# A fused residual kernel: LoRA tables and parked x on GpSimd's DMA queue, the convolution in groups of 8 channels, nine places for the first weights

## The chip, the cores and the metric

The kernel runs on one core of one Trainium2 chip. The metric is the device time in microseconds (us) of one execution; the median of several runs is compared.

## The reference, cut to what matters

`x` has shape 32 x 64 x 1024 (samples B, channels H, positions L), all in float32. Four stages each add their result to `x`:

```
x = x + conv(x)     # per channel h: causal convolution over L with a kernel K[h] made from
                    # exp, sin and 64 states per channel, plus D[h]*x, masked by each sample's length
x = x + x @ W1[id1[b]].T      # 1024 x 1024 weights chosen per sample out of 16
x = x + x @ W2[id2[b]].T      # the same, other weights
gate = x @ Wg.T + 0.5 * (x @ Ag[id3[b]].T) @ Bg[id3[b]].T      # 1024 -> 2752, rank-16 LoRA per sample
up   = x @ Wu.T + (the same with Au, Bu)
x = x + down(silu(gate) * up)                                  # 2752 -> 1024, with Ad, Bd
```

## The kernel before, in words

**Places.** `x` is kept transposed, positions on the partitions, in four chunks of 8 samples (`xs[0..3]`, 2 MB each). Chunks 2 and 3 lie in `x2pool` on the right-hand side of SBUF only until they are stored to DRAM ("parked", tile `xd`, line 129); they are loaded again later (tile `x`, line 462). All big weights go through `wpool`, nine places of 512 KB (`wa` for W1 and W2, `wf` for gate and up, `wd` for down). `early` (line 122) has four more places of 512 KB which the first four weight loads take instead, and which are used only once.

**Order of the work.** TensorE's order is the order in which the program is written (`manual_schedule(engines={PE})`). The other queues are ordered by a planner at build time, which takes the instruction written earliest among those that are ready in its own estimate; `tc.issue_after(ins)` adds that an instruction of the same queue comes after `ins`. Inside one queue everything is issued in order, and an instruction that has to wait holds up what is behind it.

**Convolution (lines 577 to 833).** `kernels(g)` makes the convolution kernels of a group of channels: GpSimd makes the products of lines 738 and 739, ScalarE takes exponentials and sines, VectorE does the range reduction and products (lines 620 to 626 and 758 to 762), TensorE multiplies 32 x 32 blocks (`pk`, line 766), ScalarE copies them to `ks` (774), VectorE adds D to one element of each (776), and two stores write them to DRAM (`kp`, 778 and 779). `convolve` takes four channels: the SP queue loads the input `uf` (787) and, for each two channels, a 1 MB Toeplitz tile `hk` out of `kp` (792); TensorE multiplies (`pc`, 804), VectorE masks into `tmp` (812), GpSimd adds into the four chunks (820). The groups are 8, 8, 16, 16 and 16 channels, and the kernels of a group are made when the convolution of the group before it has 12 channels left, or after its first four if it has 8 channels.

**Weights W1 and W2 (lines 159 to 227).** `adapters(c)` walks through one chunk: for each pair of samples and each of the two layers, 16 loads `wa` (185) and TensorE's product `pa` (191); ScalarE copies the result to `y` (201), TensorE transposes it back (`py`, 210), VectorE adds it to `x` (214). It is a generator: `yield` hands over after each half of a product (8 loads). Chunk 0 runs alone after the convolution; chunks 1 to 3 are laid between the pieces of the feed-forward of the chunk before. The loads of the first piece of chunk 0 are issued after the sixth `hk` load (line 559).

**Feed-forward (lines 369 to 557).** For each chunk, `prepare` loads the LoRA tables of gate and up (`columns`: eight DMAs on ScalarE's queue, line 259, into `raw`; one copy to `at`, line 264), forms `pl_g` and `pl_u` (285) and the combinations `xd` of `x` (362 to 366, 442). `gated` does one block of 128 hidden units: `bgu` is gathered by GpSimd (234), expanded on TensorE to `pe` (328) and copied by ScalarE to `lt` (338), which gives four PSUM banks back; then 2 x 7 half-size products `pf` (386). The result goes to `act` (421). `between` is called after each half. The table of down (`raw_d`) is also loaded by `columns`, at the start of each block of hidden units; the down products are `po` (515).

**At the seam** between chunk 0's adapters and its feed-forward, ScalarE's queue holds in this order: the last two copies of `y`, the two stores of `park` (129), the copy `at_u`, the eight loads of `raw_d`, and then the copies `lt`.

Of the kernel before, what the change touches and what calls it, by code (L numbers as in the profile page):

```python
# [8 lines left out]
F32 = mybir.dt.float32  # L9
# [2 lines left out]
ALU = mybir.AluOpType  # L12
PE = mybir.EngineType.PE
SP = mybir.EngineType.SP
ACT = mybir.EngineType.Activation

P = 128
B, H, L = 32, 64, 1024
# [7 lines left out]
FM = (FH + P - 1) // P  # L26
BLOCKS = ((0, 6), (6, FM))
MB = 6
EARLY = 4
SEG = 3  # L30
TH = TC // 2
KH = KT // 2
# [1 line left out]
NE = 16  # L34
NPIECE = 2 * BC
AT_GATED, AT_DOWN = 4, 5
GROUPS = (8, 8, 16, 16, 16)
HG = max(GROUPS)
LQ = 32
KROW = P + L  # L40

# [22 lines left out]
def kernel(  # L64
# [52 lines left out]

    right = ExitStack()
    x2pool = right.enter_context(tc.tile_pool(name="x2pool", bufs=1, side="right"))
    epool = right.enter_context(tc.tile_pool(name="epool", bufs=1, side="right"))  # L120
    late = [x_tile(x2pool, c, f"x{c}") for c in range(2, NCK)]
    early = [epool.tile([P, L], F32, tag=f"e{i}", name=f"early{i}") for i in range(EARLY)]
    blocks = convolution(tc, cst, consts, xt, xf, ssm, lens, xs + late, ps_tile)
# [2 lines left out]
    def park():  # L126
        for c, x_c in enumerate(late, 2):
            d = dpool.tile([P, KT, TC], F32, tag=f"xd{c}", name=f"xd{c}")
            nc.scalar.dma_start(d, x_c)
            parked.append(d)  # L130

    ids_sb = cpool.tile([1, 3 * B], I32, tag="ids", name="ids_sb")
# [20 lines left out]

    loads, copies = [], []
    ypool = ctx.enter_context(tc.tile_pool(name="ypool", bufs=2, reuse_waits="tile"))

    def adapter(w, layer, b0, pending):
        c, lo = b0 // BC, (b0 % BC) * H  # L160
        es = []
        for b in (b0, b0 + 1):
            with ExitStack() as after:
                if len(loads) > 1:

                    after.enter_context(tc.issue_after(loads[-2]))
                es.append(
                    nc.values_load(
                        ids_sb[0:1, layer * B + b : layer * B + b + 1],
                        engines=[SP],  # L170
                        min_val=0,
                        max_val=NE - 1,
                    )
                )
        acc = [acc_tile(f"pa{layer}_{b0}_{i}") for i in range(2)]
        for kt in range(KT):
            if kt == KH:
                yield
            if kt == (c == 0) and pending:
                residual(*pending.pop())  # L180
            wts = []
            for s, e in enumerate(es):
                name = f"wa{layer}_{b0 + s}_{kt}"
                wt = early.pop(0) if early else wpool.tile([P, L], F32, tag="w", name=name)
                load = nc.sync.dma_start(
                    wt, w[bass.ds(e, 1), kt].rearrange("e p f -> p (e f)")
                )
                wts.append(wt)
            for i in range(2):
                for s in range(2):  # L190
                    nc.tensor.matmul(  # L191
                        acc[i][s * H : (s + 1) * H, :],
                        xs[c][:, kt, lo + s * H : lo + (s + 1) * H],
                        wts[s][:, i * 512 : (i + 1) * 512],
                        start=(kt == 0),
                        stop=(kt == KT - 1),
                    )
        loads.append(load.ins)
        y = ypool.tile([P, L], F32, tag="y", name=f"y{layer}_{b0}")
        for i in range(2):  # L200
            copy = nc.scalar.copy(y[:, i * 512 : (i + 1) * 512], acc[i])
        copies.append(copy.ins)
        pending.append((c, lo, y, f"{layer}_{b0}"))
        yield

# [10 lines left out]
    def adapters(c):  # L216

        pending = []  # L220
        n = BC // 2
        for i in range(n + 1):
            if i < n:
                yield from adapter(w1, 0, c * BC + 2 * i, pending)
            if i > 0:
                yield from adapter(w2, 1, c * BC + 2 * i - 2, pending)
        residual(*pending.pop())

    hpool = ctx.enter_context(tc.tile_pool(name="hpool", bufs=1, reuse_waits="tile"))
    gpool = ctx.enter_context(tc.tile_pool(name="gpool", bufs=2, reuse_waits="tile"))  # L230

    def gather(table, c, piece, width, tag, name, bufs):
# [8 lines left out]
        )  # L241
        return t

    cols = []

    def columns(table, c, n, name):

        raw = gpool.tile([P, BC, n, R], F32, tag="raw", name=f"raw_{name}", bufs=1)
        for b in range(BC):
            with ExitStack() as after:  # L250
                if len(cols) > 3:
                    after.enter_context(tc.issue_after(cols[-4]))
                e = nc.values_load(
                    ids_sb[0:1, 2 * B + c * BC + b : 2 * B + c * BC + b + 1],
                    engines=[ACT],
                    min_val=0,
                    max_val=NE - 1,
                )
            load = nc.scalar.dma_start(
                raw[:, b], table[bass.ds(e, 1)].rearrange("e p n r -> (e p) n r")  # L260
            )
            cols.append(load.ins)
        t = gpool.tile([P, n, BC, R], F32, tag="at", name=f"at_{name}", bufs=1)
        nc.scalar.copy(t, raw.rearrange("p b n r -> p n b r"))
        return t.rearrange("p n b r -> p n (b r)")
# [94 lines left out]
        return a11, a12, s4, a22, s1, s2, a21  # L360

    def moving(b11, b12, b21, b22, t1, t2, t3, t4):
        nc.vector.tensor_sub(t3, b22, b12)
        nc.vector.tensor_sub(t1, b12, b11)
        nc.vector.tensor_sub(t2, b22, t1)
        nc.vector.tensor_sub(t4, b21, t2)
        return b11, b21, b22, t4, t1, t2, t3

    def gated(c, m, xb, between):
# [46 lines left out]
            cs.append(cq)  # L416
            between(2 * m + g)

        act = apool.tile([P, 2, TC], F32, tag="act", name=f"act_{c}_{m}")
        a = act[:n].rearrange("p i (t n) -> p (i t) n", t=2)  # L420
        nc.scalar.activation(a, cs[0][:n], AF.Sigmoid)
        nc.vector.tensor_mul(a, a, cs[0][:n])
# [23 lines left out]
    def ffn(c, xb, others):  # L446
# [10 lines left out]
                due[1] += 1  # L457

        def between(i):
            if i == 0 and c and c + 1 < NCK:  # L460
                x_n = x_tile(xpool, c + 1, "x")
                nc.sync.dma_start(x_n, parked[c - 1])
                xs.append(x_n)
            other(AT_GATED)

        for block, (m0, m1) in enumerate(BLOCKS):
# [19 lines left out]
            ab = []  # L486
            for i, act in enumerate(acts):
                k = k_of(m0 + i)
                t3 = apool.tile([P, 4, TH], F32, tag="actd", name=f"actd_{c}_{m0 + i}")
                q = [act[:k, h, t * TH : (t + 1) * TH] for h in (0, 1) for t in (0, 1)]  # L490
                ab.append(moving(*q, *(t3[:k, j] for j in range(4))))

# [63 lines left out]
                    other(AT_DOWN)  # L556
        return ready

    with tc.issue_after(blocks[5]):

        pieces = adapters(0)
        next(pieces)
    for _ in pieces:
        pass
    with tc.issue_after(copies[-1]):
        park()
    right.close()
    apool = ctx.enter_context(
        tc.tile_pool(name="apool", bufs=MB, side="right", reuse_waits="tile")
    )  # L570
    prepare(0, "g")
    xb = prepare(0, "u")
    for c in range(NCK):
# [3 lines left out]
def convolution(tc, cst, consts, xt, xf, ssm, lens, xs, ps_tile):  # L577
# [9 lines left out]
    with ExitStack() as ctx:  # L587
# [25 lines left out]
        def tt(o, a, b, op):  # L613
            nc.vector.tensor_tensor(o, a, b, op)  # L614
            return o
# [100 lines left out]

        def kernels(g):

            h0, hg = sum(GROUPS[:g]), GROUPS[g]
            shape = [P, hg, LQ]  # L720

            def over_l(ap):
                return ap[:, h0 : h0 + hg].unsqueeze(2).to_broadcast(shape)

            def over_h(at):
                return cst[:, at : at + LQ].unsqueeze(1).to_broadcast(shape)
# [2 lines left out]

            def big(tag, pool=s1):  # L730
                n[0] += 1
                return pool.tile([P, HG, LQ], F32, tag=f"b{tag}", name=f"b{tag}{g}_{n[0]}")[
                    :, :hg
                ]

            def powers(at, tag):
                theta, rho = big(f"th{tag}"), big(f"rho{tag}")
# [24 lines left out]
            tt(gt, p1, rho1, ALU.mult)  # L762

            ps = ps_tile(f"pk{g}")
            for i in range(hg):
                nc.tensor.matmul(
                    ps[:LQ, i * LQ : (i + 1) * LQ],
                    gt[:, i, :],
                    et[:, i, :],
                    start=True,  # L770
                    stop=True,
                )
            ks = s2.tile([LQ, HG, LQ], F32, tag="ks", name=f"ks{g}")[:, :hg]
            nc.scalar.copy(ks.rearrange("a h b -> a (h b)"), ps[:LQ, : hg * LQ])
            k0 = ks[0:1, :, 0]
            tt(k0, k0, dskip[0:1, h0 : h0 + hg], ALU.add)
            kp = dram.tile([hg, KROW], F32, tag=f"kp{g}", name=f"kp{g}")
            nc.scalar.dma_start(kp[:, :P], zero[:hg])
            nc.scalar.dma_start(kp[:, P:].rearrange("h (a b) -> a h b", b=LQ), ks)
            return kp  # L780

# [1 line left out]

        def convolve(kp, row, ha):

            uf = s3.tile([P, 4, KT, B], F32, tag="uf", name=f"uf{ha}")
            nc.sync.dma_start(uf, xf[:, ha : ha + 4])
            tmp = s2.tile([P, 4, KT * B], F32, tag="tmp", name=f"tmp{ha}")
            for i in range(0, 4, 2):
# [30 lines left out]
                nc.gpsimd.tensor_tensor(xv, xv, tv[:, :, c * BC : (c + 1) * BC, :], ALU.add)  # L820


        ready = kernels(0)
        ha = 0
        for g, hg in enumerate(GROUPS):
            nxt = None
            for row in range(0, hg, 4):
                convolve(ready, row, ha)
                ha += 4
                if row == max(hg - 12, 0) and g + 1 < len(GROUPS):  # L830
                    nxt = kernels(g + 1)
            ready = nxt
        return loads


# [131 lines left out]
```

## Time and profile before

| | |
|---|---|
| median of 3 runs | 2477.97 us (2476.69 to 2479.43) |
| the profiled execution's own time | 2475.95 us |
| its span in the trace | 2474.2 us |
| TensorE matmul busy | 2393.5 us (97%) |
| VectorE / ScalarE / GpSimd busy | 1116.5 / 344.5 / 130.8 us |
| moved by DMA | 500.54 MB, mean 202 GB/s |

"Busy" is the time in which an engine has an instruction running; issuing a DMA does not count. For TensorE it also holds time in which a matmul in the pipeline waits. A line of a view by groups or in order of time names the line of the program, the engine, the operation, what is written from what (`pf<-xd,wf`), the shapes and how many instructions it stands for; `SPq`, `ACTq` and `POOLq` are the queues in which an engine issues DMAs.

### The profile page before, as it was taken

What the parts mean: (1) busy time and instruction counts of PE and PEld (TensorE: products, weight loads), DVE (VectorE), ACT (ScalarE), POOL (GpSimd) and SP (SyncE); (2) the same over time, 40 slices, a digit from 0 to 9 for tenths busy, and PEclk for the clock granted to TensorE, in tenths of its full rate; (3) what the DMA queues carried; (4) which work ended last, traced back from release to release, by engine and by line L of the source; (5) the groups of instructions that cost most, each with busy time, mean ns of one, the idle gap of its engine ahead of it and who ended that gap; (6) DMA issues with size and microseconds to landing.
All of it is one profiled execution on the core that took longest, in us unless ns stands there. A gap on an engine that the chain in (4) does not pass through costs nothing.

```text
span 2474.2 us, 35037 instructions
## 1 busy us (share of the span) xinstructions
PE 2393.5 (97%) x13600; PEld 1804.0 (73%) x13600; DVE 1116.5 (45%) x2127; ACT 344.5 (14%) x656; POOL 130.8 (5%) x136
## 2 busy tenths in 40 slices
PE   3899998999999999999999999999999999999999
PEld 3895335777777787777777687777777688888887
DVE  9611003444344554444345454445345546554554
ACT  4100001111011111111011111111011102110110
POOL 3431000000000000000000000000000000000000
PEclk9999999999999999999999999999999999999999
DMA  6789997656566547655665547555655543223221
GB/s 247 253 290 356 409 409 268 246 183 225 174 225 229 183 125 261 225 204 197 203 217 212 175 139 268 213 200 203 210 206 204 181 152 117 88 69 109 94 63 62
DMA packets 176184, 500.54 MB, mean 202 GB/s; under 512 B 19794, under 2 KB 69266, under 8 KB 174994
## 3 DMA queue, kind: packets, MB, share of 16 engines
q1 hardware_dynamic: 146338, 461.82, 52.8%
q10 hardware_dynamic: 25584, 22.85, 2.8%
q0 software_dynamic: 4096, 13.63, 1.7%
q8 instruction: 107, 1.75, 0.3%
q14 instruction: 59, 0.48, 0.1%
HBM read 485.36 MB, written 12.88 MB: 201 GB/s over the span
## 4 chain that ended last, share of the span: by engine, by line
PE 88%; DMA 8%; DVE 4%; issue 0%; ACTq 0%; SPq 0%; POOL 0%; ACT 0%; DVEq 0%
PE pf L386 42%; PE po L515 22%; PE pa L191 14%; DMA wa<-in_w 5%; PE pc L804 5%; PE pe L328 2%; PE py L210 1%; PE pl_d L285 1%; DMA xd<-x 1%; PE po L311 1%; DMA x<-xd 1%; DMA out_y<-x 0%; DVE bk L620 0%; DVE bsp L614 0%; DMA wf<-in_wu 0%; PE pl_u L285 0%
## 5 line engine op out<-in xcount | busy, mean ns | idle before, releaser
L386 PE MATMUL pf<-xd,wf 128*128 128x256 f32 (+1 forms) x2816 | 670.0, 382 | 8.9 <-ACT lt L338 8.9
L386 PEld LDWEIGHTS pf<-xd,wf 128*128 128x128 f32 (+1 forms) x2816 | 523.8, 188 | 108.2 <-issue 9.7
L386 PE MATMUL pf<-xd,s 128*128 128x256 f32 (+1 forms) x2112 | 500.5, 380 | 0.3 <-DVE s L357 0.3
L191 PE MATMUL pa<-wa,x 128*64 128x512 f32 x2032 | 482.9, 598 | 12.4 <-DMA wa<-in_w 8.5
L386 PEld LDWEIGHTS pf<-xd,s 128*128 128x128 f32 (+1 forms) x2112 | 396.6, 188 | 61.9 <-issue 0.7
L191 PEld LDWEIGHTS pa<-wa,x 128*64 128x64 f32 x2032 | 147.8, 136 | 312.6 <-issue 248.6
L515 PE MATMUL po<-act,wd 128*128 128x256 f32 x704 | 177.0, 385 | 0.0
L804 PE MATMUL pc<-uf,hk 128*128 128x256 f32 (+7 forms) x1024 | 154.3, 315 | 21.1 <-DMA hk<-kp 11.9
L515 PE MATMUL po<-actd,s 128*128 128x256 f32 x704 | 173.0, 379 | 0.1
L515 PE MATMUL po<-actd,wd 128*128 128x256 f32 x704 | 172.9, 379 | 0.0
L804 PEld LDWEIGHTS pc<-uf,hk 128*128 128x128 f32 x1024 | 149.9, 197 | 25.4 <-issue 15.2
L411 DVE TENSOR_TENSOR c<-pf,u 128x256 f32<-128x256 f32 (+1 forms) x88 | 37.3, 424 | 266.5 <-PE pf L386 266.5
L515 PEld LDWEIGHTS po<-act,wd 128*128 128x128 f32 x704 | 130.3, 190 | 31.5 <-issue 8.3
L515 PEld LDWEIGHTS po<-actd,s 128*128 128x128 f32 x704 | 133.5, 190 | 18.9 <-DVE s L357 0.6
L515 PEld LDWEIGHTS po<-actd,wd 128*128 128x128 f32 x704 | 133.6, 190 | 18.4
L234 POOL DMA_INDIRECT bgu<-in_bgu,rows x44 | 46.9, 1066 | 1809.3 <-PE pe L328 1690.8
L338 ACT COPY lt<-pe 128x512 f32<-128x512 f32 (+1 forms) x176 | 90.4, 598 | 277.9 <-PE pe L328 142.1
L356 DVE TENSOR_TENSOR s<-wf 128x512 f32<-128x512 f32 x88 | 60.7, 690 | 128.9 <-DMA wf<-in_wu 56.1
L415 DVE TENSOR_TENSOR c<-c,lt 128x1024 f32<-128x1024 f32 (+1 forms) x88 | 107.5, 1222 | 5.1 <-DVE c L413 0.5
L214 DVE TENSOR_TENSOR x<-py,x 128x512 f32<-128x512 f32 x64 | 42.9, 688 | 144.1 <-PE py L210 143.9
L356 DVE TENSOR_TENSOR s<-wd 128x384 f32<-128x384 f32 x64 | 33.4, 522 | 141.5 <-PE po L515 96.7
L409 ACT COPY c<-pf 128x256 f32<-128x256 f32 (+1 forms) x88 | 32.8, 372 | 417.4 <-PE pf L386 417.4
(148 smaller groups left out, 1671.2 us busy)
## 6 DMA issues: line engine op xcount, KB each, us to landing
wa<-in_w SPq DMA_DIRECT2D x508, 512.0 KB, 7.0
wf<-in_wg SPq DMA_DIRECT2D x88, 512.0 KB, 4.0
wf<-in_wu SPq DMA_DIRECT2D x88, 512.0 KB, 4.3
wd<-in_wd SPq DMA_DIRECT2D x96, 384.0 KB, 4.1
hk<-kp SPq DMA_DIRECT2D x32, 1024.0 KB, 7.6
x<-in_xt SPq DMA_DIRECT2D x4, 2048.0 KB, 13.4
uf<-in_xf SPq DMA_DIRECT2D x16, 512.0 KB, 7.7
wd<-in_wd SPq DMA_DIRECT2D x32, 256.0 KB, 3.1
```

The source lines that it names most:

```text
L191: nc.tensor.matmul(acc[i][s * H : (s + 1) * H, :], xs[c][:, kt, lo + s * H : lo + (s + 1) * H], wts[s][:, i * 512 : (i + 1) * 512], start= ...
L214: nc.vector.tensor_add(cols, ps, cols)
L234: nc.gpsimd.indirect_dma_start(out=t, out_offset=None, in_=table, in_offset=bass.IndirectOffsetOnAxis(ap=rows[:, c, piece : piece + 1], axis=0
L328: nc.tensor.matmul(ps[:n, at_ : at_ + 2 * H], bt[pair(j), g, i, :n], tms["gu"[g]][pair(j)], start=(g + i == 0), stop=True, skip_group_chec ...
L338: nc.scalar.copy(lt[:n, :, 2 * H * j : 2 * H * (j + 1)], ps[:n].rearrange("p (i t) -> p i t", i=4),)
L356: nc.vector.tensor_add(s1, a21, a22)
L386: nc.tensor.matmul(ps, ws[j][:, kt, :n], xb[j][:, kt, :], start=start and kt == 0, stop=kt == KH - 1, skip_group_check=True,)
L409: nc.scalar.copy(cq[:n, 0], pa)
L411: nc.vector.tensor_add(cq[:n, 1], pb, u[:n])
L415: nc.vector.tensor_add(cf, cf, lt[:n, g].rearrange("p i t -> p (i t)"))
L515: nc.tensor.matmul(pss[j], ws[j][:k, i, :], ab[m - m0][j], start=(m == m0 and home[j] % 2 == 0), stop=(m == m1 - 1), skip_group_check=True,)
L804: nc.tensor.matmul(ps[:, j, d * B :], hk[:, j, d * P : (d + 1) * P], uf[:, i + j, : KT - d, :].rearrange("p k b -> p (k b)"), start=(d == ...
```

## The change

- `park` issues its two stores on GpSimd's queue, not ScalarE's, and is called later: inside `between`, after the first half of the first `gated`, after the last table load issued so far. The pool `apool` of `act` and `actd`, which takes the places of the parked chunks and of `early`, is opened there (through the list `apools`).
- `columns` reads its indices and issues its loads on GpSimd's queue.
- The convolution works in groups of 8 channels. The kernels of group 1 are made after the first four channels of group 0, those of group 2 after the last four, and from there on those of group g+2 are made when the convolution of group g ends. The tiles of a group halve in size; `uf` has two places, not three; D is added on GpSimd; `kp` and its zero border are written for eight groups, not five.
- `early` has nine places, not four; its pool is closed when chunk 0's adapters have been written down, ahead of the pools `hpool` and `gpool`. The first three pieces of chunk 0's adapters (24 loads), not one (8), are issued after the sixth `hk` load.
- `moving` makes its third difference third, not first.

```diff
-EARLY = 4
+EARLY = 9
-GROUPS = (8, 8, 16, 16, 16)
-HG = max(GROUPS)
+HG = 8
...
+    first = right.enter_context(ExitStack())
+    epool = first.enter_context(tc.tile_pool(name="epool", bufs=1, side="right"))
...
             d = dpool.tile([P, KT, TC], F32, tag=f"xd{c}", name=f"xd{c}")
-            nc.scalar.dma_start(d, x_c)
+            nc.gpsimd.dma_start(d, x_c)
...
+    with tc.issue_after(blocks[5]):
+
+        pieces = adapters(0)
+        for _ in range(3):
+            next(pieces)
+    for _ in pieces:
+        pass
+    first.close()
...
-                    engines=[ACT],
+                    engines=[POOL],
...
-            load = nc.scalar.dma_start(
+            load = nc.gpsimd.dma_start(
                 raw[:, b], table[bass.ds(e, 1)].rearrange("e p n r -> (e p) n r")
...
     def moving(b11, b12, b21, b22, t1, t2, t3, t4):
-        nc.vector.tensor_sub(t3, b22, b12)
         nc.vector.tensor_sub(t1, b12, b11)
         nc.vector.tensor_sub(t2, b22, t1)
+        nc.vector.tensor_sub(t3, b22, b12)
         nc.vector.tensor_sub(t4, b21, t2)
...
         def between(i):
+            if i == 0 and c == 0:
+                with tc.issue_after(cols[-1]):
+                    park()
+                right.close()
+                apools.append(
+                    ctx.enter_context(
+                        tc.tile_pool(
+                            name="apool", bufs=MB, side="right", reuse_waits="tile"
+                        )
+                    )
+                )
...
-    with tc.issue_after(blocks[5]):
-
-        pieces = adapters(0)
-        next(pieces)
-    for _ in pieces:
-        pass
-    with tc.issue_after(copies[-1]):
-        park()
-    right.close()
-    apool = ctx.enter_context(
-        tc.tile_pool(name="apool", bufs=MB, side="right", reuse_waits="tile")
-    )
...
-            tt(k0, k0, dskip[0:1, h0 : h0 + hg], ALU.add)
+            nc.gpsimd.tensor_tensor(k0, k0, dskip[0:1, h0 : h0 + HG], ALU.add)
...
-            uf = s3.tile([P, 4, KT, B], F32, tag="uf", name=f"uf{ha}")
+            uf = s3.tile([P, 4, KT, B], F32, tag="uf", name=f"uf{ha}", bufs=2)
...
-        ready = kernels(0)
-        ha = 0
-        for g, hg in enumerate(GROUPS):
-            nxt = None
-            for row in range(0, hg, 4):
-                convolve(ready, row, ha)
-                ha += 4
-                if row == max(hg - 12, 0) and g + 1 < len(GROUPS):
-                    nxt = kernels(g + 1)
-            ready = nxt
+        ready = [kernels(0)]
+        for ha in range(0, H, 4):
+            convolve(ready[ha // HG], ha % HG, ha)
+
+            if len(ready) < H // HG and (ha == 0 or ha % HG == 4):
+                ready.append(kernels(len(ready)))
```

More of the change, by code (lines that the diff above doesn't have):

```diff
@@ L14 @@
 SP = mybir.EngineType.SP
-ACT = mybir.EngineType.Activation
+POOL = mybir.EngineType.Pool
 P = 128
@@ L119 @@
     x2pool = right.enter_context(tc.tile_pool(name="x2pool", bufs=1, side="right"))
-    epool = right.enter_context(tc.tile_pool(name="epool", bufs=1, side="right"))
+    first = right.enter_context(ExitStack())
+    epool = first.enter_context(tc.tile_pool(name="epool", bufs=1, side="right"))
     late = [x_tile(x2pool, c, f"x{c}") for c in range(2, NCK)]
@@ L150 @@
         )
-    loads, copies = [], []
+    loads = []
     ypool = ctx.enter_context(tc.tile_pool(name="ypool", bufs=2, reuse_waits="tile"))
@@ L200, in adapter @@
         for i in range(2):
-            copy = nc.scalar.copy(y[:, i * 512 : (i + 1) * 512], acc[i])
-        copies.append(copy.ins)
+            nc.scalar.copy(y[:, i * 512 : (i + 1) * 512], acc[i])
         pending.append((c, lo, y, f"{layer}_{b0}"))
@@ L242, in gather @@
         return t
+    apools = []
     cols = []
@@ L417, in gated @@
             between(2 * m + g)
-        act = apool.tile([P, 2, TC], F32, tag="act", name=f"act_{c}_{m}")
+        act = apools[0].tile([P, 2, TC], F32, tag="act", name=f"act_{c}_{m}")
         a = act[:n].rearrange("p i (t n) -> p (i t) n", t=2)
@@ L488, in ffn @@
                 k = k_of(m0 + i)
-                t3 = apool.tile([P, 4, TH], F32, tag="actd", name=f"actd_{c}_{m0 + i}")
+                t3 = apools[0].tile([P, 4, TH], F32, tag="actd", name=f"actd_{c}_{m0 + i}")
                 q = [act[:k, h, t * TH : (t + 1) * TH] for h in (0, 1) for t in (0, 1)]
@@ L717, in kernels @@
         def kernels(g):
-            h0, hg = sum(GROUPS[:g]), GROUPS[g]
-            shape = [P, hg, LQ]
+            h0 = g * HG
+            shape = [P, HG, LQ]
             def over_l(ap):
-                return ap[:, h0 : h0 + hg].unsqueeze(2).to_broadcast(shape)
+                return ap[:, h0 : h0 + HG].unsqueeze(2).to_broadcast(shape)
             def over_h(at):
@@ L731, in big @@
                 n[0] += 1
-                return pool.tile([P, HG, LQ], F32, tag=f"b{tag}", name=f"b{tag}{g}_{n[0]}")[
-                    :, :hg
-                ]
+                return pool.tile(shape, F32, tag=f"b{tag}", name=f"b{tag}{g}_{n[0]}")
             def powers(at, tag):
@@ L764, in kernels @@
             ps = ps_tile(f"pk{g}")
-            for i in range(hg):
+            for i in range(HG):
                 nc.tensor.matmul(
@@ L772, in kernels @@
                 )
-            ks = s2.tile([LQ, HG, LQ], F32, tag="ks", name=f"ks{g}")[:, :hg]
-            nc.scalar.copy(ks.rearrange("a h b -> a (h b)"), ps[:LQ, : hg * LQ])
+            ks = s2.tile([LQ, HG, LQ], F32, tag="ks", name=f"ks{g}")
+            nc.scalar.copy(ks.rearrange("a h b -> a (h b)"), ps[:LQ, : HG * LQ])
             k0 = ks[0:1, :, 0]
-            tt(k0, k0, dskip[0:1, h0 : h0 + hg], ALU.add)
-            kp = dram.tile([hg, KROW], F32, tag=f"kp{g}", name=f"kp{g}")
-            nc.scalar.dma_start(kp[:, :P], zero[:hg])
+            nc.gpsimd.tensor_tensor(k0, k0, dskip[0:1, h0 : h0 + HG], ALU.add)
+            kp = dram.tile([HG, KROW], F32, tag=f"kp{g}", name=f"kp{g}")
+            nc.scalar.dma_start(kp[:, :P], zero)
             nc.scalar.dma_start(kp[:, P:].rearrange("h (a b) -> a h b", b=LQ), ks)
```

## The prediction

> **What bounds the kernel now.** I read the busy shares first, then the table by stretches of time, then who TensorE waited for, then the timeline around the largest wait. Columns of the table: the stretch, its length, busy us of each engine (instructions), granted TensorE clock, DMA share, GB/s.
>
> ```profile
> PE 2393.5 (97%) x13600; PEld 1804.0 (73%) x13600; DVE 1116.5 (45%) x2127; ACT 344.5 (14%) x656; POOL 130.8 (5%) x136
> ...
> 0.00:42.00 42.00, 1.38 (x17) 1.27 (x18) 37.37 (x133) 16.06 (x24) 12.63 (x16) 1.00 0.71 273
> 42.00:120.00 78.00, 68.81 (x495) 66.55 (x495) 58.10 (x89) 17.85 (x23) 35.01 (x32) 0.93 0.68 236
> 120.00:209.00 89.00, 88.93 (x643) 86.80 (x642) 13.92 (x21) 0.57 (x1) 29.21 (x36) 1.00 0.87 304
> 209.00:221.00 12.00, 10.38 (x50) 3.55 (x51) 1.62 (x3) 1.05 (x1) 5.32 (x6) 1.00 0.84 288
> 221.00:373.00 152.00, 142.81 (x526) 45.25 (x523) 9.02 (x14) 11.11 (x18) 0.00 (x0) 1.00 1.03 408
> 373.00:396.00 23.00, 10.94 (x185) 8.72 (x183) 8.73 (x12) 3.52 (x6) 0.95 (x1) 0.90 0.87 346
> ...
> 420.00:2474.00 2054.00, 2046.27 (x11600) 1575.87 (x11598) 980.10 (x1845) 288.07 (x576) 47.67 (x45) 1.00 0.52 178
> ```
>
> After 420 us TensorE is busy 2046.3 of 2054 us, and its waits there are listed as 3.2 us for `x<-xd` and 0.3 us for `s`. So nothing can be won there; a delay there would lengthen the kernel by itself. All that the change can move lies before 420, in three stages with three limits: the convolution (42 to 209), TensorE with gaps; chunk 0's adapters (209 to 373), DMA; the seam (373 to 396), a wait. These are TensorE's waits up to 420:
>
> ```profile
> PE pk L766 <- DVE bet L614: 28.7, 1, 28.7
> PE pc L804 <- DMA hk<-kp: 11.9, 1, 11.9
> PE pf L386 <- ACT lt L338: 8.9, 1, 8.9
> PE pa L191 <- DMA wa<-in_w: 8.5, 34, 1.0
> PE pc L804 <- DVE bre L624: 6.1, 1, 6.1
> PE pc L804 <- issue: 3.1, 1, 3.1
> ```
>
> The first two are the start (first product at 41.7). The 6.1 (named after VectorE, but `hk` of group 2 was issued at 87.9 and TensorE resumed at 94.0: it is that DMA) and the 3.1 (group 1) are groups whose kernels came late. The 8.9 stands in ScalarE's timeline:
>
> ```profile
> 372.74 0.82 ACTq L129 DMA_DIRECT2D xd<-x  x2
> 375.99 1.05 ACT L264 COPY at_u<-raw_u 128x1024 f32<-128x1024 f32 x1 [2.72 <-PE pl_g L285]
> 376.94 1.05 ACT L442 COPY xd<-x 128x1024 f32<-128x1024 f32 x1
> 377.06 17.65 ACTq L259 DMA_DIRECT2D raw_d<-in_ad  x8
> 394.75 1.56 ACT L338 COPY lt<-pe 128x512 f32<-128x512 f32 x3 [16.76 <-DMA raw_d<-in_ad]
> ```
>
> The eight table loads, whose issue waits on the stores ahead of them (landed at 384.4 and 391.1), keep ScalarE from copying `lt`; the third `pf` product needs a PSUM bank of `pe`, and TensorE stands from 386.5 to 395.4.
>
> [...] in 221 to 373 TensorE counts 142.8 us busy, but in the feed-forward 32 such matmuls take 7.02 us, so the stage's 512 need 112 us; the DMA share of 1.03 is the limit. [...] a 512-wide L623, 0.69 us alone, took 1.53 beside GpSimd at 47.9.
>
> **Part 1, convolution.** From 41.7 to 208.9 is 167.2 us. Needed: 128 matmuls per 8 channels take 18.44 us (55.33 per 384), `pk` 0.65 per 8 channels: 8 x 19.1 = 152.7. The surplus of 14.5 is the 6.1, the 3.1, 2.2 for the second `hk` of the first group, and about 3 of low clock (0.93). A whole group ahead removes the 6.1: group 2's `pk` comes 18.4 us before its convolution, the chain from `pk` to landed `hk` takes some 13 (before, group 1: 53.4 to 66.5). Group 1's `pk` stays 9.4 us ahead, so its wait stays, less what D's addition saves: before, that addition waited 2.5 us in VectorE's queue (`ks` copied 55.4, added 57.9). On GpSimd I take 1.5 saved (0 to 2.5, GpSimd being idle then). The same at the very start: copied 31.0, added 32.8 to 33.8; I take 1 (-1 to 2.3). Sum: 6.1 + 1.5 + 1 = 8.6, lower end 2, upper 11.
> Added work: VectorE, from the 256-wide rows, 3 x 2.54 + 5 x 0.42 = 9.7 us per group and 4 x 0.69 for the masks, 12.5 per 18.4 us of TensorE; before, 15.0 + 5.5 per 16 channels. Covered by TensorE, with 5.9 us of room per group. Three more zero stores on ScalarE's queue (0.52 each) fall before its first real work at 8.8. `uf` with two places is issued one convolution (9.2 us) ahead; `uf` and `hk` landed in 7.7 and 7.6, so the room is 1.5 us: nothing taken, up to 5 in the lower end, because early weight loads may come between.
>
> **Part 2, chunk 0's adapters.** 163.7 us from the convolution's end to the last product. A load is 0.524 MB / 408 GB/s = 1.285 us; TensorE uses one in 0.88. Before, 13 places were filled or on the way when TensorE began (210.6), then SP stood until 216.0, when the first `wpool` place came free; DMA share dropped to 0.84. Now 18 places: 5 x 1.285 = 6.4 us less to load later. But `early` is not refilled: the first `wpool` tile is now released after five steps of two loads (8.8 us), not three (5.3), so 3.5 of it goes to an idle DMA. Net 2.9; I take 3. If the five are not loaded before the convolution ends (four needed gaps in `hk`'s issue, at 79, 121 and 159, which better kernels may close), 0; if the table loads (1 MB, 2.6 us) fall into the idle time, 6.4. The tables move by the same bytes. On GpSimd they could come between the last additions to `x` and delay TensorE's start by one or two issues of 1 to 1.8 us: within these ends.
>
> **Part 3, the seam.** The stores and `raw_d` leave ScalarE's queue, `lt` is copied when `pe` is done (382.8): 8.9 gone. Next late is nothing in sight: PSUM then turns over as in later blocks. On GpSimd: eight issues, estimated 1.8 us each (gather's 1.07 plus the register work of 0.7 seen between ScalarE's), then two stores, then `bgu` of the second block: 377 + 14.5 + 3 = 395, landed (8 us under load) by 403, wanted at 421 (two halves and two adapter pieces of 19.3 after 382.8): hidden, room 18. The stores, 4.2 MB, now run beside the feed-forward's loads (10 x 0.524 MB in 19.3 us, 271 GB/s of 408) instead of a standing TensorE; nine places are 17 us of cover. I take 1 us lost (0 to 6, the latter if `act`, which takes the parked places, held ScalarE). SP too had waited 10.6 us for `xd` and 8.3 for `raw_d`; those go. Net 7.9, ends 3 and 9.
>
> **Rest.** Later chunks: `raw_u` must go between `at_g` (883) and the end of `pl_g` (907); eight issues at 1.8 plus landing end at about 900. Hidden, room 7, and the copy before `pl_u` (925) has more. ScalarE loses work that nobody waited for. `moving`: t2 1.2 us earlier, but no wait on it is listed: 0.
>
> **Sum.** 8.6 + 3 + 7.9 = 19.5. The profiled execution took 2475.95 (span 2474.2 and 1.75 around it), so 2456.4; the median is 2.0 above that execution: **2458**.
>
> **Rivals.** (a) The adapters eat the gain: loads are issued only after the last `hk`, and nine places fill at DMA's pace while extra bursts cost the convolution some us. Parts 1 and 2 give about 3 instead of 11.6: 2467. For it: the gaps in which `early` was loaded were exactly those of late kernels. Against: 24 loads are allowed from the sixth `hk` on. (b) Slower: VectorE becomes the convolution's bound. From 42 to 94 it was busy 51.6 of 52 us, with rows stretched by GpSimd, which now also gets D's addition. From 18.4 us per group on TensorE is held back; with the 11 us of parts 2 and 3 and the 9 of waits gone, it is a loss from about 21 us per group. At 24, 8 x 5 = 40 lost against 20 won: 2498. Against: my count is 12.5, and 15 with that stretching. (c) The queue moved does not release ScalarE or the tables come late every chunk: about 2476.
>
> **Chances.** Forecast 0.62, (a) 0.24, (c) 0.04, (b) 0.10. The unknown ends give 2 + 0 + 3 to 11 + 6.4 + 9: 2473 to 2451; with 1.5 us of spread of the runs (2476.69 to 2479.43) on either side, the range is 2449 to 2475, which holds the forecast and (a). A change of 0.2% (5 us) is about what can be told from none: faster 0.86, same 0.04, slower 0.10.
>
> **What would show it.** TensorE's wait `pf <- lt` gone; no wait of `pc` over 2 us after the second group; the convolution ending near 200, the adapters near 361, TensorE unbroken from about 372. Wrong: convolution ends after 209; DMA below 400 GB/s in the adapters; a wait of `pe` on `bgu` or of ScalarE on `xd`; more than 5 us of waits in the feed-forward.

## The result, and the profile after

| | median us | lowest to highest |
|---|---|---|
| before | 2478.12 | 2476.69 to 2479.43 |
| after | 2461.85 | 2460.18 to 2462.66 |

The ratio is 0.9934 (95% interval 0.9916 to 0.9951): 16 us faster, inside the range and 4 us above the forecast. (In all tables the medians are of every execution, and the ratios leave out the one slow execution on record, 4160.78 us of b1_tables_only.) The profiled execution took 2460.18 us, its span 2458.5. Cut at the starts of TensorE's instructions, the two profiled executions compare like this:

| stretch | before | after | change |
|---|---|---|---|
| start of the span to first `pc` | 41.7 | 39.4 | -2.3 |
| first to last `pc` (convolution) | 167.0 | 164.4 | -2.6 |
| last `pc` to first `pa` | 2.0 | 2.0 | 0 |
| first to last `pa` of chunk 0 (adapters) | 161.4 | 162.0 | +0.6 |
| last `pa` to first `pf` | 10.7 | 8.9 | -1.8 |
| first `pf` to the second FFN block (112 products) | 52.1 | 43.2 | -8.9 |
| the rest | 2039.3 | 2038.7 | -0.7 |

The first `pk` starts between 28.6 and 31.5 us in the profiled executions of all kernels below, and this start doesn't follow the edits; where that matters, times are counted from it.

The table by stretches of the kernel after (stretch, length, busy us of PE, PEld, DVE, ACT, POOL with instructions, granted TensorE clock, DMA share, GB/s):

```profile
39.00:120.00 81.00, 74.35 (x524) 71.93 (x525) 73.78 (x163) 24.56 (x42) 41.24 (x50) 0.96 0.69 235
120.00:204.00 84.00, 83.37 (x615) 81.22 (x613) 13.19 (x19) 1.09 (x3) 29.21 (x38) 1.00 0.87 301
204.00:216.00 12.00, 10.31 (x41) 3.33 (x42) 0.96 (x2) 0.00 (x0) 7.66 (x12) 0.86 1.03 395
216.00:368.00 152.00, 143.40 (x530) 45.39 (x526) 9.71 (x15) 11.57 (x18) 6.36 (x10) 1.00 1.03 407
368.00:396.00 28.00, 24.69 (x249) 17.81 (x250) 13.29 (x19) 9.67 (x14) 10.70 (x19) 1.00 0.89 336
```

The dip of the DMA engines behind the convolution (288 GB/s in 12 us before) is gone, 395 here; in the seam TensorE is busy 24.7 of 28 us instead of 10.9 of 23. Whom TensorE waited for in the first 420 us after (us, times, longest):

```profile
PE pc L810 <- DMA hk<-kp: 10.1, 2, 9.5
PE pa L191 <- DMA wa<-in_w: 8.0, 33, 0.9
PE pc L810 <- DVE bgt L622: 6.2, 1, 6.2
...
PE pf L395 <- ACT c L411: 1.7, 1, 1.7
...
PE pf L395 <- DVE s L366: 0.8, 1, 0.8
PE pf L395 <- DMA wf<-in_wu: 0.5, 1, 0.5
PE pe L337 <- DVE tm_u L440: 0.4, 1, 0.4
```

The wait of `pf` on `lt` is gone, and group 2's 6.1 us too. Two things are new: a wait of 6.2 us, which is group 1's `hk` (named after VectorE, but the load was issued at 62.2 and TensorE resumed at 68.6), and three small ones in the seam, for `c`, `s` and `wf`.

### The profile page after: what moved, and what is told of

The parts are those of the page before. It is cut to its first block, busy times and chain, and to the rows that moved or that the text cites. A ratio compares the mean times of both kernels' runs of the same rounds, so it can differ in the third digit from the quotient of the medians.

```text
span 2458.5 us, 35256 instructions
## 1 busy us (share of the span) xinstructions
PE 2390.5 (97%) x13600; PEld 1802.6 (73%) x13600; DVE 1124.5 (46%) x2200; ACT 351.3 (14%) x677; POOL 204.4 (8%) x286
## 3 DMA queue, kind: packets, MB, share of 16 engines
q1 hardware_dynamic: 146338, 461.82, 52.5%
## 4 chain that ended last, share of the span: by engine, by line
PE 87%; issue 6%; DMA 3%; DVE 3%; SPq 0%; POOLq 0%; POOL 0%; ACT 0%; DVEq 0%; ACTq 0%
PE pf L395 42%; PE po L535 22%; PE pa L191 13%; PE pc L810 4%; PE pe L337 2%; PE py L209 1%; PE pl_d L294 1%; PE po L320 1%; DMA x<-xd 1%; DMA wf<-in_wu 1%; DMA early<-in_w 0%; DMA out_y<-x 0%; DMA wa<-in_w 0%; DMA hk<-kp 0%; DVE bk L628 0%
## 5 line engine op out<-in xcount | busy, mean ns | idle before, releaser
L535 PE MATMUL po<-act,wd 128*128 128x256 f32 x704 | 177.0, 385 | 0.0
L535 PEld LDWEIGHTS po<-act,wd 128*128 128x128 f32 x704 | 130.3, 190 | 31.5 <-issue 8.7
```

The source lines that it names most:

```text
L535: nc.tensor.matmul(pss[j], ws[j][:k, i, :], ab[m - m0][j], start=(m == m0 and home[j] % 2 == 0), stop=(m == m1 - 1), skip_group_check=True,)
```

## The experiments

The ratios are to executions of the kernel before in the same session (medians 2477.95 to 2479.00 us). Each trace is of one execution. Diffs show the lines that matter, shortened.

### The parts alone

Four kernels take one part of the change or leave one out. a1_queues_only is before with the seam's part alone:

```diff
-            nc.scalar.dma_start(d, x_c)            # park, behind the last y copy
+            nc.gpsimd.dma_start(d, x_c)            # park, after cols[-1], in between(0)
-            load = nc.scalar.dma_start(raw[:, b], ...)
+            load = nc.gpsimd.dma_start(raw[:, b], ...)
```

> The kernel before with the seam's part of the change alone: the LoRA tables and the parked stores go through GpSimd's queue, the stores after the last table load; the convolution and the four early places are the old ones. Theory: the seam's gain stands by itself, so the wait of the first pf matmuls on lt (8.9 us) goes and the stretch from the last adapter matmul to the first matmul of the second FFN block becomes 10 to 11 us shorter (62.8 us before, 52.1 after): 2467 to 2468 us. The first pc stays at 41.7 us and the convolution at 167 us. Rival: the seam needed the emptier DMA engines that the new convolution or the five more early places leave at its start; then less than 6 us are won, over 2472 us.

Measured: 2467.80 us, ratio 0.9962 (0.9948 to 0.9975), 6 to 13 us won. The stretch from the last `pa` to the second block fell from 62.8 to 52.5 us. The seam's gain stands by itself, as expected. The adapters took 163.6 us, 2 more than before. (The new order inside `moving` is not in this kernel, and it was not tried alone.)

a2_conv_only is before with the convolution's part alone (four early places, tables and stores on ScalarE):

```diff
-GROUPS = (8, 8, 16, 16, 16)
+HG = 8
-            tt(k0, k0, dskip[0:1, h0 : h0 + hg], ALU.add)
+            nc.gpsimd.tensor_tensor(k0, k0, dskip[0:1, h0 : h0 + HG], ALU.add)
+            # uf with bufs=2; the kernels of group g + 2 are made at the end of group g
```

> The kernel before with the convolution's part alone: eight groups of 8, each kernel ahead by a whole group, two places for uf, the D addition on GpSimd; the tables and stores stay on ScalarE's queue where they were, the early places stay four. Theory: 4.9 us are won, 2.3 at the start (first pc at 39.4 us) and 2.6 in the convolution (164.4 us), and the seam keeps its 8.9 us wait on lt: 2473 us. Rival 1: the change's nine places carry the adapter stage, and with four of them it is longer than 163 us: 2475 us or more. Rival 2: GpSimd's x additions gain or lose from the tables; the convolution then ends elsewhere than at 204 us.

Measured: 2477.16 us, ratio 0.9995 (0.9987 to 1.0004): no change that can be told. The convolution did its part, the first `pa` came at 204.6 instead of 210.6. But the adapters took 167.7 us and ended at 372.3, where they had ended before (372.1). Rival 1 is right in that the adapters took the gain; whether for want of places, the next two kernels tell. a4_early4 is the changed kernel with `EARLY = 4`:

> The changed kernel with four early places instead of nine (so 13 places in all for the first adapter weights). Theory: the five more places bring nothing, because only two of the nine loads were issued before the last hk (190 us) and the rest at 190.9 to 195.5 us, when the DMA engines were free for the adapters anyway: the adapter stage keeps its 162.0 us within 1 us, and the time is 2461 to 2463 us. Rival: the nine places let 3 us of loads run ahead of TensorE; without them the adapter stage takes 165 us, 2465 us.

Measured: 2465.03 us, ratio 0.9946 (0.9932 to 0.996). The intervals of this and of the change overlap, so the runs alone don't tell them apart; in the traces the adapters end 341.7 us after the first `pk` instead of 339.0. The traces so speak against my theory (nothing), and the rival's 3 us fit. c1_conv_nine keeps convolution and nine places and puts the queues back:

```diff
-            nc.gpsimd.dma_start(d, x_c)
+            nc.scalar.dma_start(d, x_c)            # park, behind the last y copy again
-            load = nc.gpsimd.dma_start(raw[:, b], ...)
+            load = nc.scalar.dma_start(raw[:, b], ...)
```

> The changed kernel with the seam's part undone: the LoRA tables and the stores of x2 and x3 go back to ScalarE's queue and to their old place behind the last y copy; convolution and nine early places stay. Theory: with four early places the convolution's gain was given back by the adapters' loads (1 to 2 us left of 6), with nine it is kept: the adapters end 4 to 5 us earlier than before, and the seam stands as before with its wait of 9 us: 2473 to 2474 us. Rival: the seam's part is what made the adapters shorter (no table issues between the last hk and the first pa on ScalarE); then the adapters end where they did before, and 2477 us or more results.

Measured: 2477.57 us, ratio 0.9998 (0.999 to 1.0007). The rival is right: with nine places but with the old queues the adapters again took 167.2 us, and nothing was left of the convolution's gain. Of the two things put back only the tables can have done this, since the stores are issued after the last copy of `y`. What SP, which issues the weight loads, waited for in this kernel from 190 to 235 us:

```profile
SPq L185 <- DMA wa<-in_w: 9.9, 3, 4.6
SPq L185 <- DMA raw_u<-in_au: 6.7, 1, 6.7
...
SPq L185 <- DMA raw_g<-in_ag: 3.2, 1, 3.2
```

and in the changed kernel, same stretch (then one line each of the kernel before and of a1_queues_only):

```profile
SPq L185 <- PE pa L191: 12.0, 9, 4.9
SPq L185 <- DMA early<-in_w: 5.8, 6, 1.9
SPq L185 <- DMA wa<-in_w: 4.5, 8, 0.8
```

```profile
SPq L185 <- DMA raw_u<-in_au: 4.0, 2, 2.7
```

```profile
SPq L185 <- PE pa L191: 17.9, 10, 11.9
```

A weight load of SP stood 6.7 us until a table load of **ScalarE's** queue had landed (in the kernel before, two loads stood 4.0 us together); TensorE then stood 4.0 us for that `wa`. In c1_conv_nine the load stood from 224.7 us on; ScalarE could issue the first `raw_u` load only at 227.5, after its copy `at_g`, and it landed at 231.4. What ties a load of SP to a table that it does not read, no view of the profile shows.

With the tables on GpSimd no load of SP is seen to wait for a table (0 us in the view of the changed kernel, 9.9 us for `raw_u` and `raw_g` in that of c1_conv_nine); what is left are places (`pa`) and SP's own earlier loads. So the move of the tables, meant for the seam in my working, also freed the adapters' loads.

One sum holds eight kernels together. Between the last `hk` load and the last `pa` the DMA engines are the limit, so that time should be a constant, plus what the engines lost against 409 GB/s in the first 45 us (`lost us`; after these 45 us all eight move 406 to 409 GB/s), less 1.28 us (0.524 MB / 409 GB/s) for each weight load landed before:

| kernel | last `hk` issued to last `pa` | GB/s in the first 45 us | lost us | loads landed before | the constant |
|---|---|---|---|---|---|
| before | 176.9 | 358 | 5.6 | 4 | 176.4 |
| a1_queues_only | 179.1 | 339 | 7.7 | 4 | 176.5 |
| a2_conv_only | 183.1 | 326 | 9.1 | 2 | 176.6 |
| c1_conv_nine | 182.7 | 334 | 8.3 | 2 | 177.0 |
| a4_early4 | 181.2 | 348 | 6.7 | 2 | 177.1 |
| after | 177.5 | 375 | 3.7 | 2 | 176.3 |
| b3_early_spread | 177.0 | 307 | 11.2 | 9 | 177.3 |
| c2_refill | 169.6 | 366 | 4.7 | 9 | 176.4 |

(The last two come below. Of the six not in the table, b1_tables_only gives 176.5, b4_d_group0 177.6, c3_refill_d 176.4 and c4_later_d 176.2; b2_park_only 177.2, once the 10.3 us of its stores in this stretch are taken off; a3_d_on_vector fits worst, with 178.5.) The sum is bookkeeping: it shows where the time went; why the engines lost it is shown by SP's waits, where these are given. The last `hk` was issued 5.0 us sooner after the first `pk` in the changed kernel, and the adapters ended 4.4 us sooner: the convolution's gain is passed on through the loads, and only if DMA time isn't lost again.

The nine places and the tables' queue are worth little without each other. With the new convolution the engines lost 9.1 us with neither of them (a2_conv_only), 8.3 with the places alone (c1_conv_nine), 6.7 with the queue alone (a4_early4) and 3.7 with both. With the old convolution and 13 places more was lost once the tables had moved (7.7 and 8.6 us in a1_queues_only and b1_tables_only, 5.6 before): SP no longer stood for a table, but 11.9 and 12.9 us at one place that TensorE had not yet read.

### The seam's two halves

b1_tables_only is before with the tables alone on GpSimd (the second pair of lines of a1's diff), b2_park_only with the stores alone on GpSimd (the first pair, but with no order after the tables, which are then on another queue).

> The kernel before with the LoRA table loads of chunk 0 and later on GpSimd's queue; the stores of x2 and x3 stay on ScalarE's queue where they were, ahead of the FFN. Theory: the 8.9 us wait on lt came from ScalarE issuing raw_d's eight loads (1 us each) before it could copy at_d and go on to the first lt; with the loads elsewhere the wait goes even with the stores in their old place: 9 to 10 us won, 2468 to 2469 us. Rival: the stores' 4 MB on the DMA engines at the same moment were what made the tables land late, and then the wait stays for the most part: over 2473 us.

Measured: 2478.73 us, ratio 1.0004 (0.9996 to 1.0013). My theory fell. In this kernel TensorE's largest wait at the seam, and what ScalarE did:

```profile
PE pf L386 <- ACT c L402: 7.3, 1, 7.3
```

```profile
377.17 0.83 ACTq L129 DMA_DIRECT2D xd<-x  x2
...
387.79 1.07 ACT L338 COPY lt<-pe 128x512 f32<-128x512 f32 x2 [5.37 <-PE pe L328]
398.45 1.47 ACT L264 COPY at_d<-raw_d 128x1536 f32<-128x1536 f32 x1 [9.60 <-DMA bgu<-in_bgu,rows]
...
400.79 0.39 ACT L400 COPY u<-pf 128x256 f32<-128x256 f32 x1
```

The first `lt` are now copied in time, at 387.8 instead of 394.8, but the next instruction of ScalarE is the copy `at_d`. Its tables landed at 388.4 to 398.3, behind 4.2 MB of stores issued at 377 (the list names `bgu`, which landed only at 399.2), and the copies `u` and `c`, which TensorE needs, stand behind `at_d`. The wait moved from one copy to the next.

> The kernel before with the two stores on GpSimd's queue after the last table load of chunk 0; the table loads stay on ScalarE's queue. Theory: ScalarE still issues raw_d's eight loads before the first lt, only the tables land a little sooner without the stores beside them, so no more than 2 to 6 us are won: 2472 to 2476 us. Rival: the stores are the whole cause; then 9 to 10 us are won, 2468 us.

Measured: 2479.07 us, ratio 1.0002 (0.9994 to 1.001). The seam became 7.6 us shorter (55.2), a little more than my theory said. But with no table load ahead of them on GpSimd the stores were issued at 216.6 and 218.7, among the first adapter loads, and the adapters took 172.6 us. So this run doesn't tell what late stores alone are worth; it shows what the order behind the last table keeps away: stores that run beside the adapters' loads.

### The D addition, and TensorE's clock

a3_d_on_vector and b4_d_group0 are the changed kernel with D's addition back on VectorE, for all groups or for all but group 0:

```diff
-            nc.gpsimd.tensor_tensor(k0, k0, dskip[0:1, h0 : h0 + HG], ALU.add)
+            tt(k0, k0, dskip[0:1, h0 : h0 + HG], ALU.add)                         # a3
+            (nc.vector if g else nc.gpsimd).tensor_tensor(k0, k0, ..., ALU.add)   # b4
```

> The changed kernel with the D addition of all groups back on VectorE. Theory: group 1's wait of 6.2 us on hk comes from the D addition queued behind four x additions on GpSimd (ks copied at 55.6 us, D at 60.4); on VectorE the addition waits for what VectorE does of group 2 instead, so this wait becomes about 3 us, while group 0's kernel reaches memory 2 us later (first pc at 41.5 us). The two cancel within 1.5 us: 2461 to 2463 us. Rival: GpSimd isn't what makes group 1 late (the kernel's store and the load of hk are), and the wait stays at 6 us: 2464 us. Second rival: VectorE's order was what made before wait for 6 us at group 2, and that wait comes back in place of group 1's.

> The changed kernel with the D addition on GpSimd for group 0 alone and on VectorE for the other seven. Theory: group 0 keeps its gain of 2 us (GpSimd has nothing else to do then), and group 1's wait on hk becomes 3 us or less since its D addition no longer stands behind four x additions: 3 to 4 us less than the change, 2458 to 2459 us. Rival: group 1's addition stands as long behind VectorE's work for group 2 as it did behind GpSimd's: within 1 us of the change.

Measured: 2459.26 us (ratio to before 0.9931, 0.9917 to 0.9944) and 2461.29 us (0.993, 0.9917 to 0.9943). Neither can be told from the change in the runs; the traces can. GpSimd's timeline of the changed kernel, at group 1:

```profile
55.86 4.57 POOL L826 TENSOR_TENSOR x<-x,tmp 128x256 f32<-128x256 f32 x4 [1.76 <-DVE tmp L622]
60.40 0.25 POOL L782 TENSOR_TENSOR ks<-ks,par 1x8 f32<-1x8 f32 x1
```

ScalarE had copied `ks` at 55.3; the addition of eight numbers, 0.25 us long, stood behind four additions to `x` until 60.4, and the store and `hk` behind it. On VectorE it ran at 56.2, and TensorE's gap before group 1 fell from 6.4 to 2.2 us: GpSimd is the cause, the first rival of a3_d_on_vector falls. The first `pc` came 11.2 us after the first `pk` instead of 10.6 (before: 13.0), so only 0.6 of the gain at the start comes from GpSimd, not 2. The rest came on VectorE too: the store of the first `kp` was issued 3.4 us after the first `pk` in a3_d_on_vector, 2.8 in the changed kernel and 5.2 before.

The convolution of a3_d_on_vector took 158.5 us instead of 164.4, more than the gap explains. Two stretches of the changed kernel and then of a3_d_on_vector, clock in the third column from the end:

```profile
60.00:68.00 8.00, 2.34 (x30) 2.19 (x28) 7.90 (x20) 4.45 (x7) 4.31 (x7) 0.88 0.54 157
68.00:72.00 4.00, 3.42 (x11) 3.20 (x12) 3.97 (x7) 0.42 (x1) 4.00 (x4) 0.50 1.02 414
```

```profile
60.00:68.00 8.00, 6.03 (x53) 5.76 (x53) 7.86 (x20) 3.20 (x6) 3.22 (x5) 1.00 0.92 334
68.00:72.00 4.00, 4.00 (x31) 3.95 (x30) 3.93 (x8) 1.70 (x2) 3.67 (x4) 1.00 0.88 309
```

After the gap of 6.4 us the clock stood at half until 72.9, of which TensorE worked 4.3 us: by my estimate half of that, 2.1 us, lost on top of the wait. In a3_d_on_vector, after 2.2 us, it stayed at 1.00. Up to the end of the adapters such stretches at half clock were about 3.4 us long (in the kernel before, from 67.1 to 70.5), 6.8 (in the changed kernel, from 66.0 to 72.9) and 10.2 (in c1_conv_nine, from 65.8 to 76.0, where TensorE had waited 7.7 us for group 1). The traces don't show what sets the clock; short gaps were enough at times. In b4_d_group0 the gap of 2.3 us at 124.5 was followed by a stretch of 3.4,

```profile
126.00:130.00 4.00, 3.26 (x11) 3.04 (x12) 0.15 (x1) 0.00 (x0) 2.45 (x3) 0.61 1.02 409
```

and its gap of 3.3 before group 1 by another, which is why its convolution kept 163.2 us. The length of the gap alone doesn't decide. Between the last `pc` and the first `pa` TensorE stands 1.97 us, from start to start, in thirteen of the fourteen kernels; in nine of them, the changed one among them, 3.4 us at half followed, in four, the kernel before among them, none. These are the 6 us around that gap's end in the changed kernel and in the kernel before:

```profile
204.00:210.00 6.00, 4.31 (x13) 1.32 (x14) 0.96 (x2) 0.00 (x0) 5.10 (x8) 0.72 1.02 408
```

```profile
210.00:216.00 6.00, 5.38 (x26) 1.92 (x28) 0.05 (x1) 0.00 (x0) 5.06 (x6) 1.00 0.74 248
```

### Where early loads go

b3_early_spread writes the nine early loads between the loads of the convolution:

```diff
         for ha in range(0, H, 4):
             convolve(ready[ha // HG], ha % HG, ha)
+            first_weights(ha)      # from ha = 24 on, loads early[k], one each time
```

> The changed kernel with the nine early loads written out between the loads of the convolution, from row 24 on, so that all nine are issued before the last hk instead of two. Theory: the nine places bring nothing in the changed kernel because their loads come too late; with all nine landed at the first pa, seven loads (3.7 MB, 9 us at the 409 GB/s of the adapter stage) are out of the stage that the DMA engines set: the adapter stage takes 156 us or less instead of 162, 2454 to 2456 us, if the convolution keeps its 164.4 us. Rival 1: the loads take the place of hk and uf on the DMA engines, and the convolution becomes longer by as much as the adapters become shorter: 2460 to 2463 us. Rival 2: TensorE or ScalarE and not the DMA engines set the adapter stage; it stays at 162 us.

Measured: 2459.74 us, ratio to before 0.993 (0.9917 to 0.9943), as the change within the intervals. All nine were issued well before the last `hk` (the ninth 8.6 us), the convolution kept its length (163.1), and yet the adapters took 161.6 us. None of the three theories had this reason; the table by stretches of this kernel shows it:

```profile
198.00:204.00 6.00, 4.84 (x35) 4.63 (x34) 2.06 (x6) 0.00 (x0) 0.35 (x1) 1.00 1.02 414
204.00:210.00 6.00, 5.47 (x18) 1.75 (x20) 0.00 (x0) 0.00 (x0) 6.00 (x10) 0.72 0.60 227
210.00:216.00 6.00, 6.00 (x30) 2.01 (x28) 0.00 (x0) 0.00 (x0) 2.30 (x4) 1.00 0.16 49
216.00:222.00 6.00, 6.00 (x29) 1.64 (x26) 0.00 (x0) 2.12 (x3) 0.97 (x1) 1.00 0.87 305
```

By 205 all eighteen places were full, TensorE read the nine early ones first, and those take no new load; the DMA engines had nothing to do. SP stood 14.2 us for the first `wpool` place. c2_refill lets chunk 0's loads go round over all eighteen places, c3_refill_d adds a3's edit, and c4_later_d puts `raw_d` and `at_d` of the first block after its first half:

```diff
-                wt = wpool.tile([P, L], F32, tag="w", name=name)
+                wt = next_place(c, name)     # c2: nine of wpool, nine of epool, in turn, for c == 0
-            nc.gpsimd.tensor_tensor(k0, k0, ...)
+            nc.vector.tensor_tensor(k0, k0, ...)                                  # c3
+            # c4: in between(0) of chunk 0, ahead of park():
+            held.append(columns(ad[:, 0, :, :n0], 0, n0, "d0_0"))
```

> The kernel with nine early loads spread over the convolution (b3_early_spread), in which chunk 0's adapter loads also go round over all eighteen places, so that an early place is filled again as soon as TensorE has read it, instead of lying empty. Theory: in b3_early_spread the DMA engines moved 227, 49 and 305 GB/s in 204 to 222 us, 9.5 us of their 410 GB/s lost, because all eighteen places were full and the nine early ones, read first, took no new load; with the refill these 9.5 us are used, the adapters end near 357 us and the time is 2450 to 2452 us. Rival 1: the restart is bound by TensorE's pace at the first products, and then 3 us at most are won: 2457 us. Rival 2: the adapter stage ends when the tables or the first FFN weights have passed too, and they only move: no gain, 2460 us.

> c2_refill with the D addition on VectorE for all groups (as in a3_d_on_vector). Theory: group 1's wait falls from over 4 us to about 2 and TensorE's clock stays at 1.00 after it, so the convolution ends 4 to 5 us sooner; the adapters, bound by the DMA engines, keep some 3 us of it: 3 us under c2_refill. Rival: with the early loads out of the way the DMA engines alone set the adapters' end, and it doesn't move: within 1 us of c2_refill.

> c3_refill_d with the table loads raw_d of chunk 0's first block, and ScalarE's copy at_d that waits for them, put after the first half of the first FFN block instead of ahead of it. Theory: the new wait of the changed kernel's seam (TensorE 2.05 us at the third pf, for ScalarE's copies u and c that stand behind at_d) goes: 1 to 2 us under c3_refill_d. Rival: the later tables push the stores and the second block's bgu later, or the copy at_d stands before another copy that TensorE needs: 0 to 3 us over c3_refill_d.

Measured: 2462.24 us (ratio to before 0.9934, 0.992 to 0.9948), 2462.36 (0.9931, 0.9917 to 0.9944), 2465.27 (0.9944, 0.9931 to 0.9958). The refill did what it should: adapters 154.1 us instead of 161.6. But from the last `pa` to the first `pf` it now took 20.3 us instead of 8.9. Two waits of GpSimd in c2_refill from 205 to 380 us, and TensorE's longest from 200 to 390:

```profile
POOL bd L277 <- DMA wa<-in_w: 123.8, 1, 123.8
POOL raw_u L303 <- ACT at_g L308: 23.1, 1, 23.1
```

```profile
PE pl_u L329 <- ACT at_u L308: 8.1, 1, 8.1
```

The gather `bd` stood 123.8 us in GpSimd's queue until adapter loads were done, and was issued at 343.9; in the changed kernel, at 217.3. But it was not the last that held up the tables `raw_u` behind it. They waited another 23.1 us for ScalarE's copy `at_g`, which stood behind the last copies of `y` and came at 366.6 instead of 222.1, though its own tables had landed by 221.9. So `raw_u` was issued at 368.0 instead of 223.4, and TensorE waited for it. The trace doesn't say why `bd` waits for `wa` and why `at_g` was ordered so late; that their buffers lie where early places were is a likely reason, not one that was tried. c3_refill_d shows the same (adapters 152.8, then 19.8); its gap before group 1 was 4.0 us instead of 2.2. In the traces its second block starts 2.8 us sooner after the first `pk` than that of c2_refill, but in the medians nothing of the 3 us expected is seen. In c4_later_d the wait of `pf` on `c` is gone as expected, but the next one, on `s`, is 1.5 us instead of 1.1; the first block changed by 0.2 us, and the time is no better. No kernel measured can be told from the change as faster.

## Why the prediction was right, and where its sum was not

The direction, the size and the main mechanism held: the seam was to give most of what is sure, and did. That the sum came within 4 us of the time is in part luck: against the traces the seam was 2.8 us too low, the convolution 3.7 and the adapters 3.6 too high. Its three terms went like this.

**Seam, predicted 7.9, in the trace 10.7.** "8.9 gone" is right, but "next late is nothing in sight" failed twice. `at_d` stood ahead of `u` and `c` (2.05 us at the third product), and `wf` and `s` came late, with 1.05 and 1.17 us from start to start. Together this is 3.3 us above what stands there otherwise (0.22 between products, 0.52 from `pa` to `pf`), where I took 1. Against it stood a term that I left out: in the kernel before, the clock was at half for 6.2 us after TensorE resumed (0.50 from 392 to 400), by the same estimate 3.1 us lost. And 1.8 us came from the wait on `tm_u`, which goes with the stores off ScalarE's queue (8.9 us from `pa` to `pf` in every such kernel but the three with the refill; 10.7 to 11.2 with the stores on it). The wait on `lt` itself was 9.1 above the usual spacing, and 9.1 + 3.1 + 1.8 - 3.3 = 10.7. The estimate of 1.8 us for a table load on GpSimd was three times too high for the eight of the first block: 0.54 to 0.59 us each, at a pace of 0.6 to 1.2, so they took 7 us and not 14.5. The eight of the second block, later at the seam, did come 1.2 to 2.1 us apart.

**Convolution, predicted 8.6, in the trace 4.9.** Group 2's 6.1 went, as worked out. The step that failed is "on GpSimd I take 1.5 saved, GpSimd being idle then": it was in the middle of four additions to `x`, the addition came 4.8 us late instead of 2.5, and the gap before group 1 grew from 3.4 to 6.4. At the very start, where I took 1, 2.3 came, by a3_d_on_vector only 0.6 of it through the addition on GpSimd. What I named as 3 us of low clock is no term of its own: a stretch at half clock followed each of the two gaps before groups 1 and 2 (3.4 and 6.8 us long), and in the changed kernel the longer gap before group 1 brought 2.1 us of it back. VectorE did not become the bound: from the fourth group on the `pk` follow each other every 19.1 us, TensorE's own pace. (Two slips changed nothing: the lower end of 2 is not the sum of its own ends, 6.1 + 0 - 1 - 5 = 0.1; and, under "Rest", `pl_g` starts at 907 and ends at 908.8.)

**Adapters, predicted 3, in the trace -0.6.** The nine places are worth about 3 us when the tables are on GpSimd (a4_early4, in the trace), but not by "18 places instead of 13 when TensorE begins". Only two loads had landed before the last `hk`, where before it had been four: better kernels close the gaps in which they ran, which is rival (a)'s mechanism, and two loads are 2.6 us. The other early loads ran behind the last `hk` and kept the DMA engines busy while SP would have stood. That the tables on ScalarE's queue hold SP's weight loads was not in my working here, though it lists the same kind of wait for `raw_d` at the seam; and the tables' move to another queue saved more than ScalarE's time of issue, since SP's waits for them went with it (9.9 us in c1_conv_nine, none in the changed kernel). c1_conv_nine shows that without that move neither convolution nor places would have brought anything: that the gain got through at all is luck. I added three parts that are not additive: alone the seam gives about 10 and the convolution nothing, and together it is 16.

## What to carry to other kernels

Ask of every gain ahead of a transfer-bound stage by which loads it reaches that stage's end; here the convolution's 5 us were passed on only when the queues and the places let the loads run on without a pause. When a queue's head is moved away, write down the next three instructions behind it and what each waits for: the tables alone and the stores alone moved the wait from `lt` to `at_d`, or time into another stage, and gained nothing. Before a short instruction is put on an idle-looking engine, look at what that engine does at that moment, not at its share of the span.

## What the runs showed of the hardware

A gap in TensorE's work cost more than its length here: after 6.4 us the clock was at half for another 4.3 us of work in the changed kernel (an estimated 2.1 us lost), after 9.3 us for 6.2 in the kernel before (3.1 lost). Gaps of about 2 us went either way: the same 1.97 us was followed by 3.4 us at half clock in nine kernels and by none in four. What that cost at the start of the adapters no run tells.

A load in one queue stood for a load in another whose data it does not read: a weight load of SP stood 6.7 us in c1_conv_nine until a table load of ScalarE's queue had landed, and two stood 4.0 us together in the kernel before. What ties them was not shown; in the changed kernel and in a1_queues_only, with the tables on GpSimd's queue, this wait is not seen.
